# Selective-scan kernel: the running sum y is added by TensorE through the identity, and copied back by ScalarE, in images 1 to 3 as well as in image 0

## The chip, the cores and the metric

The kernel runs on one core of one Trainium2 chip. The metric is the device time in microseconds (us) of one execution, taken as the median of several. Five engines of the core matter: TensorE (PE in the profile, its weight loads PEld), VectorE (DVE), ScalarE (ACT), GpSimd (POOL) and SyncE (SP), which only issues DMAs here. Each engine runs its own instructions in the order of the program; semaphores make one engine wait for another.

## The reference, cut to what matters

Layer 0 is a selective scan over four images of 48 x 48 positions with 256 channels. For each image, each of four directions k (rows, columns, and both reversed) and each of 16 states n, a recurrence runs along the L = 2304 positions, and the four results are added in the order of the positions:

```
dA = jnp.exp(dt_l[..., None] * A)
h  = h * dA + (dt_l * u_l)[..., None] * B_l[:, :, None, :]
y  = jnp.einsum('bkdn,bkn->bkd', h, C_l)
...
ys = ys + Ds.reshape(1, K, d, 1) * xs
y  = ys[:, 0] + ys[:, 2][..., ::-1]        # + directions 1 and 3, transposed
```

Layer norm, a gate and a projection follow, then attention over the tokens, then a long convolution with 16 filters (the "STU"), whose products are matrix multiplications.

## The kernel before, in words

**Scan stage.** Each image b has one scan stage. It is cut into 24 chunks: 4 directions times 6 chunks of CS = 384 positions. A chunk has 8 units (h, q): two halves h of the channels, four groups q of four states. One unit is a tile `s` of 128 partitions x 4 x 384 (partitions hold 32 channels x 4 states). Its steps, with lines of the profile:

- L517 `s = rep * B`: on DVE for five units of a chunk (B is first copied by ACT into a PSUM slot, L509), on POOL for the three units in `POOLED`.
- L526 decay: ACT writes exp(dt * A) into a slot of `ring`, four slots in PSUM (five in image 0), four decays per unit.
- L533 scan: DVE runs the recurrence over 384 positions, four scans per unit; a scan frees its ring slot for a later decay.
- L541 and L543: POOL saves the last column as `carry` and multiplies `s` by C.
- L551: PE sums over the states with the matrix `csum`, for two units at a time; after the four q of a half the bank `y` (one buffer) holds the chunk's result of 128 channels x 384 positions.
- `add_y`: the result goes into `ya` (`yaccs` in the code), the running sum of the image in SBUF. This is what the change touches. There are two per chunk, 48 per image.

**Preparing later chunks.** While a chunk is scanned, `prep` makes dt and dt * u of the next ones: matmuls of PE into ring slots (L421, L438), copies by ACT (L428, L441), softplus by ACT in place (L452, issued for two chunks one behind the other, so in every second chunk), and L474 on DVE, two products `dx = dt * x` of 128 x 384, followed by the DMAs that store and replicate them (L463, L468, SP's queue). Column directions (odd k) read `x` and `ya` with a stride.

**Other work beside the scans.** In image 0 PE makes the mixed filters G (L984). In images 1 to 3 PE runs the STU of the image before: products L1207 into the banks cx and cy, projections L1273; ACT copies the results between (L1223, L1227, L1230, L1231). The function `more` hands this work out in equal shares of columns, in four places per unit; the result copies come 500 columns later in the program.

**Order.** Nothing is planned by a scheduler: the Python loop in `scans` writes the order of every engine by hand. Step s of the loop enters later units, runs the four scans of unit s with shares of the other work between them, and lets POOL multiply unit s - 1. The sums L551 of units s - 3 and s - 2 end a step; `add_y` of a finished half comes in the next step. `fill` issues as many decays as ring slots are free ahead of each scan.

In image 0 the addition was already in the form that the change extends: PE adds `ya` onto the sums through `ident` (L554), and ACT copies the bank back (L561). In images 1 to 3 DVE adds the bank to `ya` (L563).

Of the kernel before, what the change touches and what calls it, by code (L numbers as in the profile page):

```python
# [10 lines left out]
ALU = mybir.AluOpType  # L11
# [10 lines left out]
CS = 384  # L22
SUB = 384
NT = L // P
G4, DL, C4, Q4 = 4, 32, 4, 4
# [35 lines left out]
def hybrid_kernel(ctx: ExitStack, tc: tile.TileContext, a: dict, out: bass.AP):  # L61
# [3 lines left out]
    nc = tc.nc  # L65
# [272 lines left out]
    def in_order(t, k, lo, n):  # L338

        if k % 2 == 0:  # L340
            return t[:, lo // W:(lo + n) // W, :]
        return t.rearrange("p h w -> p w h")[:, lo // H:(lo + n) // H, :]
# [154 lines left out]
    class Unit:  # L497
# [47 lines left out]
        def sum_c(self, ps):  # L545

            ch = self.ch
            if self.q == 0:
                ch.y = ps.tile([P, 512], F32, tag="y", name=f"y{self.name}")
            for g in range(G4):  # L550
                nc.tensor.matmul(ch.y[g * DL:(g + 1) * DL, :CS], csum, self.s[:, g], start=(self.q == 0),  # L551
                                 stop=(self.q == Q4 - 1))
            if ch.b == 0 and self.q == Q4 - 1:
                nc.tensor.matmul(ch.y[:, :CS], ident, in_order(yaccs[ch.b][self.h], ch.k, ch.lo, CS), start=False,  # L554
                                 stop=True, skip_group_check=True)

        def add_y(self):
            ch = self.ch
            v = in_order(yaccs[ch.b][self.h], ch.k, ch.lo, CS)
            if ch.b == 0:  # L560
                nc.scalar.copy(v, ch.y[:, :CS].rearrange("p (r w) -> p r w", w=v.shape[2]))  # L561
                return
            nc.vector.tensor_tensor(v, v, ch.y[:, :CS].rearrange("p (r w) -> p r w", w=v.shape[2]), ALU.add)  # L563

    NCH = L // CS
    POOLED = ((0, 3), (1, 1), (1, 3))
# [50 lines left out]
    def scans(b, chunks, preps, front, sp, back, ring, finish, work, work_cols):  # L617

        units = [Unit(ch, h, q) for ch in chunks for h, q in quads]
        total = len(chunks) * CHUNK_COLS + work_cols  # L620
        done = [0]

        def more(share):

            while done[0] < share * total:
                cols = next(work, None)
                if cols is None:
                    break
                done[0] += cols

        def enter(s):

            if s + 2 < len(units) and units[s + 2].pool:
                units[s + 2].enter(sp.s, ring)
            if 0 <= s + 1 < len(units) and not units[s + 1].pool:
                units[s + 1].enter(sp.s, ring)

        wanted, issued = [], [0]

        def fill(left=0):  # L640

            while wanted and ring.free:
                wanted.pop(0).spread(ring)
            while len(ring.free) > left and issued[0] < G4 * len(units):
                i = issued[0]
                issued[0] += 1
                units[i // G4].decay(i % G4, ring)

        def scan(s, g):
            fill()  # L650
            units[s].scan(g, ring)

        def spread(s):
            if s < len(units) and not units[s].pool:
                wanted.append(units[s])

        def prepare(s):

            ci, j = divmod(s, len(quads))
            for c in range(ci + 1, ci + 5):  # L660
                if c < len(chunks) and 0 <= s - len(quads) * c + LEAD[c % 2] < STEPS[c % 2]:
                    done[0] += next(preps[c]) or 0

        def refill(s, i):

            if 0 <= s < len(units) and s // len(quads) + 1 < len(chunks):
                u, nxt = units[s], chunks[s // len(quads) + 1]
                if u.h == NH - 1:
                    nxt.fetch(i + u.q, front)

        pending = []
        spread(0)
        fill(len(ring.free) - 1)
        enter(-2)
        enter(-1)
        spread(1)
        fill(1)
        for i in range(3 if units[0].ch.b else 0):
            done[0] += next(work)
        for s in range(len(units) + 2):  # L680
            real = s < len(units)
            enter(s)
            prepare(s)
            if real:
                scan(s, 0)
            more((s + 0.25) / len(units))
            next(finish, None)
            if 1 <= s <= len(units):
                units[s - 1].times_c(s >= len(units) - (units[0].ch.b == 0))
            if real:  # L690
                scan(s, 1)
            if pending:
                pending.pop().add_y()
            prepare(s)
            more((s + 0.5) / len(units))
            next(finish, None)
            spread(s + 2)
            if real:
                scan(s, 2)
            more((s + 0.75) / len(units))  # L700
            next(finish, None)
            prepare(s)
            if real:
                scan(s, 3)
            refill(s - 2, Q4)
            refill(s + 1, 0)
            if s >= 2 and units[s - 2].q % 2:
                units[s - 3].sum_c(back.psy)
                units[s - 2].sum_c(back.psy)
                done[0] += 2 * CS  # L710
                if units[s - 2].q == Q4 - 1:
                    pending.append(units[s - 2])
            more((s + 1) / len(units))
            next(finish, None)
        for u in pending:
            u.add_y()
        for _ in work:
            pass
# [898 lines left out]
    for b in range(B):  # L1617
# [3 lines left out]
        if b == 0:  # L1621
            mixed = Stage(tc, "m", "right", two=(2, SB))
            scans(b, *first, front, sp, ps, ring, iter(()), mixture(mixed, ps), MIX_COLS)
            mixed.close()
        else:
            env.append(ps)
            scans(b, *first, front, sp, ps, ring, finish(b - 1), work, STU_COLS)
# [139 lines left out]
```

## Time and profile before

| what | value |
|---|---|
| median of 3 runs | 5423.6 us (5423.21 to 5428.04) |
| profiled execution | 5427.03 us; its span 5425.3 us |
| mean granted TensorE clock | 0.926 |
| busy share of the span | PE 86%, PEld 58%, DVE 80%, ACT 59%, POOL 67% |
| scan stage, first scan to last: image 0 | 111.9 to 1059.3 us |
| scan stage, first scan to last: image 1 | 1295.4 to 2250.8 us |

A row of the profile gives the line, the engine, the operation, the tiles (output <- inputs), the shape and the count; then the busy time in us, the mean of one in ns, and the idle time of the engine just before these instructions with what ended it. A float32 matmul of this kernel stands as two matmul instructions (192 of them would be 96 products); the end of a matmul is modelled. Overlapping instructions of one engine are counted once in busy time. Images 2 and 3 repeat image 1 closely: windows of 834 us in each show the same counts within four instructions on every engine.

### The profile page before, as it was taken

The numbers are of one execution on the slowest core, as the hardware profiler recorded it, in microseconds if no ns is written. First come the engines' busy times: TensorE is split into PE (matmuls) and PEld (weight loads), VectorE is DVE, ScalarE is ACT, GpSimd is POOL, SyncE is SP. The second block draws the span as 40 slices with busy tenths as digits, with TensorE's granted clock in tenths as the row PEclk, the third lists the DMA queues.
The fourth block names the chain that finished last, engine by engine and source line by source line (L and its number), as shares of the span: only waits on it lengthen the run. The fifth ranks groups of instructions, "written<-read, shape, count | busy, mean of one in ns | idle before, by whom it ended". The sixth has DMA issues, their size and how long they took to land. (4 is left out here: it accounts for less than half of the span.)

```text
span 5425.3 us, 71267 instructions
## 1 busy us (share of the span) xinstructions
PE 4658.1 (86%) x23372; PEld 3120.5 (58%) x23372; DVE 4324.9 (80%) x5309; ACT 3210.7 (59%) x6846; POOL 3656.8 (67%) x1881
## 2 busy tenths in 40 slices
PE   4555555599999999998899999898899999989999
PEld 2222222255666666645666666656666667559987
DVE  8999999856999999856999999658999999423211
ACT  3666666546777766456776766457777666432111
POOL 2999999713989999605999999407998999201100
PEclk7777777799999999999999999999999999999999
DMA  4444454404877777406787787227777777136543
GB/s 138 154 162 155 160 171 160 128 27 145 247 260 253 252 260 244 146 31 204 237 264 249 243 272 247 88 78 211 248 246 260 248 260 238 38 83 153 151 142 91
DMA packets 732185, 996.11 MB, mean 184 GB/s; under 512 B 108969, under 2 KB 580649, under 8 KB 731753
## 3 DMA queue, kind: packets, MB, share of 16 engines
q1 hardware_dynamic: 725992, 988.26, 57.6%
q10 hardware_dynamic: 5824, 3.30, 0.3%
q8 instruction: 187, 3.06, 0.2%
q14 instruction: 182, 1.48, 0.1%
HBM read 873.03 MB, written 118.31 MB: 183 GB/s over the span
## 5 line engine op out<-in xcount | busy, mean ns | idle before, releaser
L533 DVE TENSOR_TENSOR_SCAN s<-ring,s 128x385 f32<-128x385 f32 x3072 | 2691.4, 937 | 75.8 <-ACT ring L526 75.4
L543 POOL TENSOR_TENSOR s<-s,bc 128x1536 f32<-128x1536 f32 x763 | 2423.2, 3178 | 96.3 <-DVE s L533 39.9
L526 ACT ACTIVATE ring<-rep,A 128x384 f32<-128x384 f32 x3072 | 1757.8, 584 | 885.5 <-DVE s L517 524.2
L517 POOL TENSOR_TENSOR s<-rep,bc 128x1536 f32<-128x1536 f32 x288 | 994.2, 3452 | 131.9 <-DMA rep<-dtdud 70.9
L517 DVE TENSOR_TENSOR s<-rep,ring 128x1536 f32<-128x1536 f32 x480 | 830.3, 1731 | 34.9 <-ACT ring L509 20.0
L551 PE MATMUL y<-s,csum 128*32 128x384 f32 x6144 | 646.9, 538 | 109.4 <-POOL s L543 88.9
L1207 PE MATMUL cx<-tt,u 128*128 128x252 f32 (+7 forms) x2880 | 622.5, 361 | 124.3 <-ACT cy L1223 123.3
L1207 PEld LDWEIGHTS cx<-tt,u 128*128 128x128 f32 x2880 | 514.9, 195 | 308.0 <-ACT cy L1223 181.3
L1207 PE MATMUL cx<-tt,us 128*128 128x252 f32 (+7 forms) x2880 | 597.6, 352 | 51.5 <-ACT U L1231 49.4
L1207 PEld LDWEIGHTS cx<-tt,us 128*128 128x128 f32 x2880 | 494.6, 191 | 172.6 <-ACT U L1231 73.0
L1207 PE MATMUL cy<-tt,u 128*128 128x252 f32 (+5 forms) x2880 | 588.2, 349 | 0.0
L1207 PEld LDWEIGHTS cy<-tt,u 128*128 128x128 f32 x2880 | 497.2, 192 | 102.6 <-issue 41.1
L984 PE MATMUL G<-M,W 128*128 128x256 f32 (+3 forms) x512 | 222.7, 570 | 259.5 <-ACT W L974 134.7
L551 PEld LDWEIGHTS y<-s,csum 128*32 128x32 f32 x6144 | 166.3, 116 | 457.6 <-issue 259.0
L1273 PE MATMUL pr<-U,G 128*128 128x288 f32 (+4 forms) x1344 | 425.6, 448 | 3.0 <-DMA G<-gd 3.0
L1543 POOL TENSOR_TENSOR t<-s,s 128x512 f32<-128x512 f32 x48 | 63.4, 1320 | 513.8 <-ACT s L1541 513.8
L866 ACT ACTIVATE e<-s,shift 128x512 f32<-128x512 f32 (+1 forms) x360 | 230.2, 643 | 272.1 <-PE s L864 271.7
L864 PE MATMUL s<-xnT 128*128 128x512 f32 (+1 forms) x720 | 339.7, 556 | 23.7 <-ACT xnT L824 12.5
L856 PE MATMUL o<-e,xn 128*128 128x512 f32 (+1 forms) x720 | 336.9, 552 | 0.0
L984 PEld LDWEIGHTS G<-M,W 128*128 128x128 f32 x512 | 111.4, 239 | 364.0 <-ACT W L974 142.1
L1273 PEld LDWEIGHTS pr<-U,G 128*128 128x128 f32 x1344 | 235.0, 192 | 121.8 <-issue 71.4
L541 POOL COPY carry<-s 128x4 f32<-128x4 f32 x640 | 121.0, 189 | 231.9 <-DVE s L533 229.5
(237 smaller groups left out, 5040.6 us busy)
## 6 DMA issues: line engine op xcount, KB each, us to landing
rep<-dtdud SPq DMA_DIRECT2D x768, 384.0 KB
bc<-xdd SPq DMA_DIRECT2D x768, 192.0 KB
tt<-fd SPq DMA_DIRECT2D x144, 577.0 KB
tt<-fd SPq DMA_DIRECT2D x144, 451.0 KB
tt<-fd SPq DMA_DIRECT2D x144, 325.0 KB
dtdud<-dt SPq DMA_DIRECT2D x192, 192.0 KB
dtdud<-dx SPq DMA_DIRECT2D x192, 192.0 KB
t<-fd SPq DMA_DIRECT2D x80, 384.0 KB
```

The costliest lines, as they stand in the source:

```text
L517: eng.tensor_tensor(s, self.ch.rep[self.h][:, :, 1], bt.unsqueeze(1).to_broadcast([P, G4, CS]), ALU.mult)
L526: nc.scalar.activation(ring.body(self.dA[g]), ch.rep[self.h][:, g, 0], AF.Exp, scale=A[:, ch.k, self.h * G4 + g, self.q:self.q + 1])
L533: nc.vector.tensor_tensor_scan(s, ring.decays(i, ch.rev), s, 0.0, ALU.mult, ALU.add)
L541: nc.gpsimd.tensor_copy(carry[:, self.h, self.q].unsqueeze(2), self.s[:, :, end:end + 1])
L543: eng.tensor_tensor(self.s, self.s, ch.bc[Q4 + self.q].unsqueeze(1).to_broadcast([P, G4, CS]), ALU.mult)
L551: nc.tensor.matmul(ch.y[g * DL:(g + 1) * DL, :CS], csum, self.s[:, g], start=(self.q == 0), stop=(self.q == Q4 - 1))
L856: nc.tensor.matmul(po[J][:, :w], xn[:, i], e[:, :w], start=(i == 0), stop=(i == NT - 1))
L864: nc.tensor.matmul(p[:, :w], xnT[:, i * P:(i + 1) * P], xnT[:, 512 * J:512 * J + w], start=True, stop=True)
L866: nc.scalar.activation(e[:, :w], p[:, :w], AF.Exp, bias=shift)
L984: nc.tensor.matmul(p[:, :n], W[:, q if t else 0, i], M[t][:, i].unsqueeze(1).to_broadcast([P, n, C]), start=(t == 0 and i == 0), stop=(t = ...
L1207: nc.tensor.matmul(p4[:, 1:3, v - (hi - at):] if g else p4[:, 0:4:3, v - (hi - at):], x, t[:, :, hi - 1 - at + J * P:end if end >= 0 else ...
L1273: nc.tensor.matmul(o if q else o.rearrange("p f r m -> p r f m"), G, U[n][:, 4 * q:4 * q + 4, v0:v1].rearrange("p (a b) m -> p a b m", a=2 ...
```

## The change

`add_y` of images 1 to 3 takes the form that image 0 has: one more product of PE per half and chunk, of `ya` with the identity onto the bank, and a copy by ACT from the bank to `ya`; the addition by DVE is gone. In images 1 to 3 the place of `add_y` in a step moves from behind scan 1 to behind scan 3. Image 0 stays as it is. The instructions of POOL and the DMAs of SP keep their order.

```diff
-            if ch.b == 0 and self.q == Q4 - 1:
+            if self.q == Q4 - 1:
                 nc.tensor.matmul(ch.y[:, :CS], ident, in_order(yaccs[ch.b][self.h], ch.k, ch.lo, CS), start=False,
                                  stop=True, skip_group_check=True)
 
         def add_y(self):
             ch = self.ch
             v = in_order(yaccs[ch.b][self.h], ch.k, ch.lo, CS)
-            if ch.b == 0:
-                nc.scalar.copy(v, ch.y[:, :CS].rearrange("p (r w) -> p r w", w=v.shape[2]))
-                return
-            nc.vector.tensor_tensor(v, v, ch.y[:, :CS].rearrange("p (r w) -> p r w", w=v.shape[2]), ALU.add)
+            nc.scalar.copy(v, ch.y[:, :CS].rearrange("p (r w) -> p r w", w=v.shape[2]))
...
             if real:
                 scan(s, 1)
-            if pending:
+            if pending and not units[0].ch.b:
                 pending.pop().add_y()
...
             if real:
                 scan(s, 3)
+            if pending:
+                pending.pop().add_y()
             refill(s - 2, Q4)
```

## The prediction

> **What bounds the kernel now.** I read the page first, then busy time by window inside the scan stages, then the waits of each engine, then the timeline where those waits sit. The page names no single bound: DVE 80%, PE 86%, POOL 67% are averages over unlike stages. The change acts in three scan stages of about 955 us, so I take a steady stretch of image 1 and the like-long one of image 0 (columns: PE, PEld, DVE, ACT, POOL busy, clock, DMA share, GB/s):
>
> ```profile
> 150.00:985.00 835.00, 462.63 (x2008) 177.94 (x2006) 801.38 (x822) 569.71 (x1227) 768.60 (x377) 0.75 0.49 162
> 1345.00:2180.00 835.00, 785.09 (x4447) 562.41 (x4445) 809.50 (x865) 596.76 (x1306) 766.49 (x375) 0.98 0.78 252
> ...
> 1782.00:2180.00 398.00, 382.12 (x2104) 271.16 (x2102) 385.85 (x414) 275.68 (x591) 367.40 (x183) 0.98 0.76 253
> ```
>
> In 835 us DVE is busy 97%, PE 94%, POOL 92%. DVE looks like the bound. But image 0, where DVE no longer adds y, does the same POOL work in the same time (377 against 375 instructions), so taking this addition from DVE need not quicken the chunks. The timeline at the end of a chunk shows why:
>
> ```profile
> 1455.59 3.18 POOL L543 TENSOR_TENSOR s<-s,bc 128x1536 f32<-128x1536 f32 x1
> ...
> 1456.90 2.75 DVE L474 TENSOR_TENSOR dx<-dt,xc 128x384 f32<-128x384 f32 x2
> ...
> 1459.58 0.95 DVE L533 TENSOR_TENSOR_SCAN s<-ring,s 128x385 f32<-128x385 f32 x1
> ...
> 1460.59 0.19 POOL L541 COPY carry<-s 128x4 f32<-128x4 f32 x1 [1.82 <-DVE s L533]
> ```
>
> Two L474 need about 1.0 us (530 ns is the shortest), but took 2.75: DVE was held until POOL's product ended at 1458.77. Then POOL idled 1.82 us, because its next unit needs the scan behind L474. Once per chunk DVE thus waits for POOL and POOL for DVE. A chunk costs POOL eight L543 (3.18), three L517 (3.45), up to eight carries (0.19) with their 0.08 us gaps, 37.9 us less some overlap, and this 1.82: about 39.2 us, or 39.7 where the two L474 last 0.8 us each. Image 1 spends 955 / 24 = 39.8. **POOL's chain with this meeting is a floor just below the present pace; DVE's addition is not.**
>
> The waits of that stretch:
>
> ```profile
> POOL carry L541 <- DVE s L533: 45.1, 23, 3.2
> POOL s L543 <- DVE s L533: 11.4, 5, 3.9
> ...
> DVE s L533 <- ACT ring L526: 15.9, 16, 2.3
> DVE ya L563 <- PE y L551: 8.3, 11, 1.9
> ...
> PE cx L1207 <- ACT cy L1223: 31.5, 21, 4.1
> PE cx L1207 <- ACT U L1231: 14.6, 11, 2.9
> ```
>
> POOL waits 56.5 us for DVE. The meeting explains 21 x 1.82 = 38, plus about 11 chunks x 0.53 for the slow L474 = 44. Only some 12 us per image are late DVE.
>
> **What the Trainium skill says.** "SBUF — State Buffer", section "Who interferes with whom", says that a VectorE instruction with two SBUF inputs contends with a GpSimd instruction that reads SBUF, one with at most one does not, and PE and ACT never wait. The trace agrees: L474 (two SBUF inputs) stretches to 2.28 us at 1456.90 and 3.26 at most, while L563, with y in PSUM, stays within 0.52 to 0.87. So the new copy and product join no such queue, and the removed addition stood in none. "ScalarE activation tables: per-element evaluation and per-set limits", section "What a function is on this engine", puts two functions of different table sets one load of 1283 ns apart; the trace has exactly that, twice around each pair of softplus, and DVE starves behind it:
>
> ```profile
> 1495.03 1.28 ACT L526 ACT_TABLE_LOAD   x1
> ...
> 1496.94 1.81 DVE L533 TENSOR_TENSOR_SCAN s<-ring,s 128x385 f32<-128x385 f32 x2 [2.11 <-ACT ring L526]
> ```
>
> **The change part by part,** per image of 48 additions: the groups of both forms (x144 are three images, x48 is image 0), and the product in image 0's timeline.
>
> ```profile
> L563 DVE TENSOR_TENSOR ya<-ya,y 128x384 f32<-128x384 f32 x144 | 98.5, 684 | 31.2 <-PE y L551 30.9
> L561 ACT COPY ya<-y 128x384 f32<-128x384 f32 x48 | 31.0, 646 | 43.4 <-PE y L554 43.3
> ```
>
> ```profile
> 714.69 0.91 PE L554 MATMUL y<-ya,ident 128*128 128x384 f32 x2
> 715.44 1.45 PE L984 MATMUL G<-M,W 128*128 128x384 f32 x4
> ```
>
> DVE loses 48 x 0.684 = 33 us of instructions and 31 / 3 = 10 us of waits for y. Not all shortens the chunk: the ceiling is the 12 us in which POOL waits beyond the floor. In every second chunk DVE starves on the softplus before it reaches L474, and arriving earlier only lengthens that wait; by the timeline about a third of the 12 us lies there. **Gain: 8 us.**
>
> PE gains a product from 714.69 to 715.44, 0.75 us at full clock: 48 x 0.75 = 36 us. It fills PE's own waits for ACT (46 us in the stretch), which shrink when PE is later. In the second half (1782 to 2180) those are 15.7 us and the 20 products cost 15.0: full. The planner's column count does not include them, so nothing is taken away in exchange. Estimate for lag left uncovered there: **2 us**, from 0 to 15.
>
> ACT gains 48 x 0.646 = 31 us, inside 238 us of idle. Two things behind it count. First, queued decays: the place behind scan 3 comes about 1.5 us later in ACT's order than DVE's old one (one scan, one decay of 0.58), y comes 0.75 later, so waits for y, up to 1.9 before, stay near 1.2, and two or three scans of decays are ahead. Only behind the softplus is none ahead: the changed order puts the copy between the first and second decay, which makes the second some 0.3 us late, ten times per image, half of it hidden by L474's own hold: **1.5 us**, from 0 to 8. Second, results of L1207 arrive up to 0.75 us later at ACT, which already waits 43 us for them (21.7, 13.7 and 8.0 for L1230, L1223, L1227); where this delays a softplus, DVE pays. Four such delays of 0.75: **3 us**, from 0 to 10.
>
> At the image's end the last y must pass the product too before the means L746: **0.8 us**, the copy itself (0.82 to 0.84) equalling the addition (0.83). The single bank y is free one step before its next sums, at no cost; if ACT held it, PE would wait (5.8 us once in image 0). `add_y` issues no DMA, so its move passes nothing on SP or POOL.
>
> Sum: -8 + 2 + 1.5 + 3 + 0.8 = -0.7 us per image, -2 in all. Against the profiled 5427.0 that is 5425; the median of the runs lies 3.4 lower, so I predict **5421.5 us**.
>
> **The rivals.** *A, the relief counts in full:* PE's waits swallow the products and nothing moves on ACT. For it: 46 us of PE waiting, 238 of ACT idle. Against it: the second half and the softplus. Gain 8 to 12 per image: about 5394, and 5387 at the very best (3 x 12).
>
> *B, PE becomes the bound, slower:* place, the second half of each scan stage, where conv products stand nearly back to back. If its 15.7 us of waiting are forced (PE waits there for a copy that hangs on a decay, that hangs on a scan), the products add 15 us per image; ACT, queued behind later conv results, passes it to the ring and DVE. With a gain of 5 in the first half, +10 per image: 5454. It decides from the point where less than about half of that waiting can be filled. At worst no wait is filled anywhere, 3 x 36: 5531. Against it: DVE tolerates PE's lateness by two scans.
>
> *C, the change does less than it says:* image 0 untouched and PE's clock already 0.98, so no further effect there; this merges with my forecast.
>
> **How the numbers follow.** A measurement of this kernel can tell about 0.2%, 11 us, from no change. Forecast (gain and losses cancel, own range 5406 to 5440): 0.40, of which 0.28 within 11 us and 0.06 on either side. A: 0.24, all faster but 0.01. B: 0.36, all slower but 0.02. Sums: faster 0.29, same 0.31, slower 0.40. The range must reach into A and B: 5396 leaves out A's far half (0.1), 5466 leaves out B beyond a third of the 3 x 36 us (0.1).
>
> **What would show it right or wrong.** Right: L563 gone; L554 four times as many; per chunk still 39.2 to 39.8 us; POOL's wait per chunk still 1.82 or 2.35; L474 held longer, as in image 0 (up to 3.26). PE waits for ACT fall by most of 36 us. A: POOL's waits in 1345 to 2180 fall towards 44 us and the stage to 943. B: PE over 98% in the second half, ACT's waits for PE (43 us) doubled, the ring waits of DVE (15.9) doubled, POOL's waits above 65. The forecast is wrong if a scan stage moves by more than 6 us.

## The result, and the profile after

The changed kernel takes **5475.8 us** (median of 4 runs, 5474.05 to 5479.49) against 5423.4 for the kernel before beside it: 1.0094 times as long, with a 95% interval of 1.0081 to 1.0106. It is slower by 52 us; the forecast was 5421.5 and its range ended at 5466. Its form is close to that of rival B. The profiled execution has a span of 5472.3 us at a mean granted clock of 0.932, so the loss is not one of the clock (0.926 before).

The same two windows of image 1, of the kernel after (columns: PE, PEld, DVE, ACT, POOL busy with counts, clock, DMA share, GB/s):

```profile
1345.00:2180.00 835.00, 803.21 (x4471) 568.42 (x4472) 775.42 (x815) 611.26 (x1332) 758.66 (x371) 0.99 0.78 250
1782.00:2180.00 398.00, 389.81 (x2117) 273.37 (x2117) 368.94 (x389) 280.72 (x600) 361.14 (x179) 0.99 0.76 250
```

In the second half PE is now busy 389.8 of 398 us, 98%, while DVE and POOL are less busy than before: POOL did 371 instructions in 835 us where it had done 375. DVE and POOL do less work in the same time and PE is fuller; ACT is busier too, by its new copies.

The waits in 1345 to 2180 of the kernel after (us in total, number, longest), in the order POOL, DVE, ACT, PE:

```profile
POOL carry L541 <- DVE s L533: 52.8, 20, 5.1
POOL s L543 <- DVE s L533: 11.2, 5, 6.0
...
DVE s L533 <- ACT ring L526: 41.4, 32, 3.9
...
ACT cy L1222 <- PE cx L1206: 35.2, 23, 3.6
ACT U L1229 <- PE cx L1206: 30.4, 26, 3.5
ACT U L1226 <- PE cy L1206: 13.7, 16, 2.0
ACT ya L560 <- PE y L554: 1.5, 2, 1.2
...
PE cx L1206 <- ACT cy L1222: 16.4, 11, 3.8
PE cx L1206 <- ACT U L1230: 10.8, 6, 2.7
```

(Lines behind the change stand one lower than before: L1206 was L1207.) PE's waits for ACT fell from 46 to 27 us. But ACT's waits for PE rose from 43 to 79, DVE's waits for a decay from 15.9 to 41.4, and POOL's for a scan from 56.5 to 64.0. Not all of the longer waits for a decay goes with the loss: in the first experiment below, without the product and without a loss, they are 31.5 us already, so only some 10 us come with the product. Over the whole of the three scan stages POOL's waits for scans rose from 204.0 to 248.8 us, 45 of the 51 us by which the stages grew. One place in the timeline of the kernel after shows how the lateness travels:

```profile
1533.17 0.91 PE L554 MATMUL y<-ya,ident 128*128 128x384 f32 x2
...
1536.99 0.56 ACT L1222 COPY cy<-cx 128x504 f32<-128x504 f32 x1 [3.62 <-PE cx L1206]
...
1537.56 0.59 ACT L526 ACTIVATE ring<-rep,A 128x384 f32<-128x384 f32 x1
...
1538.26 0.96 DVE L533 TENSOR_TENSOR_SCAN s<-ring,s 128x385 f32<-128x385 f32 x1 [2.64 <-ACT ring L526]
...
1541.18 1.58 DVE L474 TENSOR_TENSOR dx<-dt,xc 128x384 f32<-128x384 f32 x2
...
1543.77 3.18 POOL L543 TENSOR_TENSOR s<-s,bc 128x1536 f32<-128x1536 f32 x1 [6.00 <-DVE s L533]
```

The same place in the kernel before:

```profile
1534.38 0.56 ACT L1223 COPY cy<-cx 128x504 f32<-128x504 f32 x1 [2.97 <-PE cx L1207]
...
1535.64 2.66 DVE L533 TENSOR_TENSOR_SCAN s<-ring,s 128x385 f32<-128x385 f32 x3 [0.38 <-ACT ring L526]
...
1540.81 3.18 POOL L543 TENSOR_TENSOR s<-s,bc 128x1536 f32<-128x1536 f32 x1 [3.88 <-DVE s L533]
```

PE makes the new product ahead of the long convolution's products. ACT, whose next instruction in order is the copy L1222 of such a result, waits 3.62 us for it. The decay L526 stands behind that copy and the trace shows no wait of its own, so the scan waits 2.64 us, and POOL at the end of the row 6.00 us. The three waits were there before, at 2.97, 0.38 and 3.88 us: the product lengthens them. Against the kernel before, PE is 1.97 us later at the sums ahead of the product and 2.72 us later behind it; the copy comes 2.61 us later, the scan 2.62, and POOL's product 2.96, while POOL's last work ahead of its wait had started only 0.82 us later.

Where in a stage the time went, from the starts of the scans in the traces (mean per image of images 1 to 3, us; a stage has 24 chunks):

| kernel | chunk 0 | 1 to 11 | 12 to 21 | 22 and 23 | stage |
|---|---|---|---|---|---|
| before | 47.2 | 439.5 | 396.9 | 71.8 | 955.4 |
| after | 48.2 | 443.1 | 404.3 | 76.7 | 972.3 |
| after without the product (first experiment below) | 47.5 | 437.0 | 396.4 | 71.6 | 952.5 |

The stage moved by 17 us, where the prediction called itself wrong from 6. 16.9 us per image are 51 in all: the whole loss lies in the three scan stages, and 12 of the 17 us behind chunk 11: 7.4 in chunks 12 to 21, where PE had been fullest (96%), and 4.9 in the last two.

### The profile page after: what moved, and what is told of

It reads as the page before. It is cut to its first block, busy times and chain, and to the rows that moved or that the text cites. A ratio compares the mean times of both kernels' runs of the same rounds, so it can differ in the third digit from the quotient of the medians.

```text
span 5472.3 us, 72019 instructions
## 1 busy us (share of the span) xinstructions
PE 4752.1 (87%) x23660; PEld 3164.1 (58%) x23660; DVE 4241.2 (78%) x5165; ACT 3279.5 (60%) x6990; POOL 3657.6 (67%) x1881
## 5 line engine op out<-in xcount | busy, mean ns | idle before, releaser
L526 ACT ACTIVATE ring<-rep,A 128x384 f32<-128x384 f32 x3072 | 1755.0, 584 | 706.0 <-DVE s L517 422.3
L551 PE MATMUL y<-s,csum 128*32 128x384 f32 x6144 | 634.6, 530 | 114.4 <-POOL s L543 82.2
L1206 PE MATMUL cx<-tt,u 128*128 128x252 f32 (+7 forms) x2880 | 606.3, 355 | 80.2 <-ACT cy L1222 79.4
L1206 PEld LDWEIGHTS cx<-tt,u 128*128 128x128 f32 x2880 | 512.6, 193 | 250.8 <-ACT cy L1222 120.4
L1206 PE MATMUL cx<-tt,us 128*128 128x252 f32 (+7 forms) x2880 | 599.3, 353 | 40.3 <-ACT U L1230 38.3
L1206 PEld LDWEIGHTS cx<-tt,us 128*128 128x128 f32 x2880 | 504.3, 194 | 157.4 <-ACT U L1230 57.4
L1206 PE MATMUL cy<-tt,u 128*128 128x252 f32 (+5 forms) x2880 | 581.4, 346 | 0.0
L1206 PEld LDWEIGHTS cy<-tt,u 128*128 128x128 f32 x2880 | 498.3, 191 | 100.3 <-issue 42.0
```

Of the source, the lines that this page charges most:

```text
L526: nc.scalar.activation(ring.body(self.dA[g]), ch.rep[self.h][:, g, 0], AF.Exp, scale=A[:, ch.k, self.h * G4 + g, self.q:self.q + 1])
L1206: nc.tensor.matmul(p4[:, 1:3, v - (hi - at):] if g else p4[:, 0:4:3, v - (hi - at):], x, t[:, :, hi - 1 - at + J * P:end if end >= 0 else ...
```

## The experiments

**Theory 1**: the product on PE costs the time, since PE's waits for ACT could not be filled, and its lateness passes through ACT's order to DVE and POOL. **Rival**: the copy on ACT costs it, by delaying decays. Each experiment was timed beside the kernel before, whose median then lay between 5423.7 and 5425.2 us; times of different experiments are compared on that ground. The first four ask which part it is.

### The copy alone

`add_y` and its place are those of the changed kernel; images 1 to 3 get no product, so the old y is left out of their sum.

```diff
-            if self.q == Q4 - 1:
+            if ch.b == 0 and self.q == Q4 - 1:
```

> The changed kernel without the product by TensorE in images 1 to 3: ScalarE still copies the bank to ya behind scan 3, VectorE adds nothing, so in those images the old y is left out of the sum. Theory 1 (the product makes TensorE late; ScalarE waits for the later convolution results and with it the decays): with TensorE's load as before, the relief of VectorE remains alone, 5385 to 5412 us. Theory 2 (the copy on ScalarE starves the ring of decays): nearly all of the loss stays, 5460 to 5476 us. Theory 3 (the place of the copy): like theory 2.

Measured: 5418.7 us, ratio 0.9989 [0.9981, 0.9998]. Without the product the loss is gone: the 48 copies per image on ACT cost next to nothing, and the product costs 57 us. The range expected of theory 1 was missed all the same, by 7 us, because the relief of DVE brings less than it took.

### The product alone, copied by DVE in the old place

The kernel before with the product in all images:

```diff
-            nc.vector.tensor_tensor(v, v, ch.y[:, :CS].rearrange("p (r w) -> p r w", w=v.shape[2]), ALU.add)
+            nc.vector.tensor_copy(v, ch.y[:, :CS].rearrange("p (r w) -> p r w", w=v.shape[2]))
```

> The product by TensorE in all images, but in images 1 to 3 VectorE copies the bank back, in its old place behind scan 1; ScalarE has no new work. Theory 1: TensorE is as late as in the changed kernel and VectorE is not relieved, 5465 to 5510 us. Theory 2: VectorE works as before and ScalarE too, 5415 to 5432 us. Theory 3: as theory 2.

Measured: 5486.7 us, 1.0113 [1.0098, 1.0128]. The loss stays although ACT has no copy, so the rival falls. By the medians it is 11 us worse than the changed kernel, though the two intervals overlap. DVE itself now stands behind the product (waits in 1345 to 2180 of this kernel):

```profile
DVE ya L563 <- PE y L554: 30.2, 27, 3.8
```

That wait was 8.3 us before. DVE's waits for a decay are 15.7 us here, as in the kernel before (15.9). The product's lateness thus reaches DVE mainly by another way than in the changed kernel and costs as much: that the product costs the time is shown, while the way through ACT's order is read from the trace of the changed kernel.

### No addition at all

The kernel before without L563 in images 1 to 3: what freeing DVE can bring at most.

> The kernel before without the addition in images 1 to 3 (y is not added to ya at all): no product, no copy, nothing on VectorE. This measures what the relief of VectorE can bring at most. The floor of the prediction (GpSimd's chain with one meeting per chunk) says 8 to 12 us per image: 5385 to 5400 us. If VectorE itself is the bound (its 97% in the window), it is 33 us of additions plus 10 us of waits per image: 5295 to 5330 us.

Measured: 5416.9 us, 0.9983 [0.9976, 0.9990]: a gain of 7 to 9 us in the whole kernel, though DVE lost 98.5 us of instructions. The groups show where the rest went, first in the kernel before:

```profile
L533 DVE TENSOR_TENSOR_SCAN s<-ring,s 128x385 f32<-128x385 f32 x3072 | 2691.4, 937 | 75.8 <-ACT ring L526 75.4
...
L474 DVE TENSOR_TENSOR dx<-dt,xc 128x384 f32<-128x384 f32 x192 | 171.7, 934 | 4.6 <-ACT dt L452 4.6
```

and in this kernel:

```profile
L533 DVE TENSOR_TENSOR_SCAN s<-ring,s 128x385 f32<-128x385 f32 x3072 | 2679.8, 938 | 116.8 <-ACT ring L526 116.5
...
L474 DVE TENSOR_TENSOR dx<-dt,xc 128x384 f32<-128x384 f32 x192 | 211.5, 1141 | 4.6 <-ACT dt L452 4.6
```

L474 lasted 934 ns in the mean before and lasts 1141 here, with the same shapes: 40 us more busy time. The scans wait 117 us for decays instead of 75. This fits a DVE that reaches L474 earlier, is held there longer, and runs into the ring. So DVE's addition did not set the pace. The gain is smaller even than the floor of the prediction allowed: 5385 to 5400 us were expected of it.

### The old place

The changed kernel with the copy behind scan 1:

```diff
-            if pending and not units[0].ch.b:
+            if pending:
                 pending.pop().add_y()
...
-            if pending:
-                pending.pop().add_y()
```

> The changed kernel with the copy by ScalarE behind scan 1 in images 1 to 3 too, as image 0 has it. Theory 1: the place matters little or makes it worse, as ScalarE then waits for y itself: 5470 to 5520 us. Theory 3 (the place behind scan 3, just behind the restart after softplus, is what costs): 5424 to 5450 us. Theory 2: within 10 us of the changed kernel.

Measured: 5483.4 us, 1.0106 [1.0091, 1.0121], some 8 us more than the changed kernel, with overlapping intervals. In its window ACT waits 30.0 us for the product (`ACT ya L560 <- PE y L554: 30.0, 25, 4.1`), against 1.5 in the place behind scan 3. The move takes this wait away; that it saves time is not shown beyond the noise.

### How much of the product: half, and twice

In images 1 to 3 the product covers 192 of 384 columns (the rest of the old y is left out), or is issued twice (the old y then counts double).

```diff
-                nc.tensor.matmul(ch.y[:, :CS], ident, in_order(yaccs[ch.b][self.h], ch.k, ch.lo, CS), start=False,
+                n = CS if ch.b == 0 else CS // 2
+                nc.tensor.matmul(ch.y[:, :n], ident, in_order(yaccs[ch.b][self.h], ch.k, ch.lo, n), start=False,
```

```diff
+                for i in range(2 if ch.b else 1):
+                    nc.tensor.matmul(ch.y[:, :CS], ident, in_order(yaccs[ch.b][self.h], ch.k, ch.lo, CS), start=False,
+                                     stop=True, skip_group_check=True)
```

> The changed kernel with the product over half of the columns (192 of 384) in images 1 to 3, so the old y is left out for the other half. TensorE then has 0.36 to 0.4 us per product for 0.75. Theory 1b with TensorE full throughout: half of the 57 us, 5443 to 5451 us. Theory 1a or TensorE full only in some chunks: the first half of the load is cheaper, as waits take it up: 5424 to 5440 us.

> The changed kernel with the product issued twice in images 1 to 3 (ya then counts double in the sum). From none over half to one product the time went 5419, 5442, 5476. If TensorE is then full in every chunk, the second product passes on with its whole 0.75 us x 144 = 108 us: 5570 to 5590 us. If half of every load is still taken up by waits: some 57 to 70 us more, 5530 to 5548 us.

Measured: half 5441.8 us, 1.0033 [1.0023, 1.0043]; twice 5586.1 us, 1.0301 [1.0284, 1.0319]. The table sets them beside the load on PE. A product's load is read from the trace as the time from its start to PE's next product; it is given here for all three images. Waits are those in 1345 to 2180, summed from the answers as above.

| product | load on PE | time | ACT for PE | DVE for the ring | POOL for DVE |
|---|---|---|---|---|---|
| none (copy alone) | 0 | 5418.7 | 41.8 | 31.5 | 53.9 |
| half | 83 | 5441.8 | 62.5 | 37.4 | 59.4 |
| whole (the change) | 152 | 5475.8 | 79.3 | 41.4 | 64.0 |
| twice | 291 | 5586.1 | 114.7 | 60.2 | 93.0 |

The first 83 us of load cost 23 us, 0.28 per us; the next 69 cost 34, 0.49 per us; the last 139 cost 110, 0.79 per us. Half a product already costs time, so the load is not free up to a point, and each further us costs more, four fifths of it in the last step. The half lies between the two ranges that were expected of it; the doubled product lies in the range for a PE that is full in every chunk. The windows of the kernel with two products:

```profile
1345.00:2180.00 835.00, 805.77 (x4416) 562.57 (x4416) 745.01 (x784) 590.27 (x1289) 729.75 (x356) 0.99 0.76 241
1782.00:2180.00 398.00, 391.57 (x2091) 272.19 (x2084) 352.61 (x371) 269.35 (x578) 345.43 (x169) 1.00 0.74 241
```

PE's busy time hardly rises over the 803.2 and 389.8 of the change: it was nearly full already there, and now POOL's count falls from 371 to 356.

### A lighter PE, before and after

Part of the projection L1273 (its second product group, for 9 of 16 filters) is left out, in the kernel after and in the kernel before. L1273's busy time falls from 425.6 to 319.1 us in the latter:

```diff
-                for v0, v1, x in parts(w, extra):
+                for v0, v1, x in () if q and (k % 2 or k in (4, 12)) and k < KF - 1 else parts(w, extra):
```

> The changed kernel with other work taken from TensorE instead: in images 1 to 3 the projection of the second filter bank is left out for 9 of 16 filters (part of the sum is missing in the output), some 36 us of matmuls per image, as much as the products are; they stand spread over the stage, away from the products. If what counts is the sum of TensorE's load: the loss is gone, 5412 to 5432 us. If it is the place of the products: it stays, 5455 to 5476 us.

> The kernel before with the same projections left out. If TensorE was a bound before already and its load passes on at the same rate of about half (57 us for 108 us): 5424 less some 40 to 55, 5370 to 5385 us. If the floor of the prediction holds (GpSimd's chain with one meeting per chunk, some 12 us per image under the time before): not under 5387 us, and rather 5400 to 5420.

Measured: after 5450.5 us, 1.0048 [1.0033, 1.0063]; before 5432.8 us, 1.0014 [1.0007, 1.0021]. The same relief brings 25 us after the change and none before it (there it is 8 us slower; why was not tested). The waits of PE in the second of these, in 1345 to 2180:

```profile
PE cx L1207 <- ACT cy L1223: 45.0, 28, 4.2
PE cx L1207 <- ACT U L1231: 18.6, 16, 3.1
```

They sum to 64 us where the kernel before has 46: PE without the work just waits longer. So PE did not bound the kernel before, and with the product it does in part; this and the table of doses carry theory 1. Both ranges for the kernel after were missed, as were those for the kernel before. With the lighter PE the change still costs 18 us. The relief, some 107 us of L1273, is less than the 152 us of the products, so a rest was due; whether that is all of the reason stays open.

### Is it the distance of the copies, or the count?

If PE is late, results could be taken later: `LATER`, the distance of the result copies in columns, from 500 to 750, in both kernels. Or the product's columns could be counted, so that `more` hands out less work beside it.

```diff
-LATER = 500
+LATER = 750
```

```diff
-        total = len(chunks) * CHUNK_COLS + work_cols
+        total = len(chunks) * (CHUNK_COLS + NH * CS) + work_cols
...
+                    done[0] += CS
```

> The changed kernel with LATER = 750 for 500: ScalarE's copies of the convolution results stand 250 columns later in its order. The runs so far put the loss on the product by TensorE (57 us with it, none without). Theory 1a (ScalarE meets those copies too early, because TensorE is late by the product, and its decays stand behind them): the copies come when the result is there, ScalarE's waits for it (79 us in the window) fall by half, and 15 to 40 us come back: 5435 to 5460 us. Theory 1b (TensorE has no room left: throughput): TensorE now waits longer for the copies in turn, no gain: 5470 to 5495 us.

> The kernel before with LATER = 750 for 500, as control. Theory 1a: ScalarE's waits for convolution results there (43 us in the window) fall, but they cost little: 5412 to 5426 us. Theory 1b: TensorE waits longer for the copies: 5424 to 5445 us.

> The changed kernel, with the columns of the product counted in the shares by which other work is handed to TensorE, so that less of it follows directly on a product. Theory 1a: a smoother load, up to 15 us back: 5460 to 5476 us. Theory 1b: the sum of the work is the same, within 6 us of the changed kernel: 5470 to 5482 us.

Measured: later in the kernel after 5496.0 us, 1.0127 [1.0110, 1.0144]; later in the kernel before 5464.9, 1.0072 [1.0057, 1.0087]; counted 5466.5, 1.0075 [1.0057, 1.0092]. The idea that a later copy relieves the chain fell: it costs 20 us after and 41 us before, above every range given for it. ACT's waits for PE hardly fall (79.3 to 77.7 in the window after), and PE waits longer for its banks (27 to 35 us). In the kernel before ACT's waits for PE fall from 43.4 to 36.5 us, but PE's for ACT rise from 46.1 to 52.2 and DVE's for y from 8.3 to 18.8: PE and ACT hand banks to and fro, and there the wait that one is spared turns up with others. Counting gives some 9 us back, though its interval overlaps that of the change.

### What the product costs: columns, rows, and its place

The trace of the kernel after shows that products are not alike. The first product here belongs to a column direction (the last chunk of k = 1) and 20 us later to a row direction:

```profile
1795.19 1.54 PE L554 MATMUL y<-ya,ident 128*128 128x384 f32 x2
1796.56 1.69 PE L1206 MATMUL cx<-tt,u 128*128 128x254 f32 x8
...
1814.74 0.91 PE L554 MATMUL y<-ya,ident 128*128 128x384 f32 x2
1815.48 1.66 PE L1206 MATMUL cy<-tt,u 128*128 128x252 f32 x8
```

From its start to the next product it takes 1.37 us in the one and 0.74 in the other; the medians over an image are 1.36 and 0.75. The kernel before had shown it too, in the column directions of image 0:

```profile
373.23 1.54 PE L554 MATMUL y<-ya,ident 128*128 128x384 f32 x2
374.59 1.68 PE L984 MATMUL G<-M,W 128*128 128x512 f32 x4
```

In column directions the product reads `ya` with a step of 48 values, 192 bytes. The Trainium skill, page "SBUF — State Buffer", section "Door 1: The DMA port swizzle (why `[64,N]` ≈ `[32,N]`)", says that SBUF has lines of 16 bytes and that every access that crosses to a new line pays. The experiment reads the same values in runs of 8 neighbours, and lets the output carry the step instead:

```diff
+                y, v = ch.y[:, :CS], in_order(yaccs[ch.b][self.h], ch.k, ch.lo, CS)
+                if ch.b and ch.k % 2:
+                    y, v = y.rearrange("p (w h) -> p h w", h=H), v.rearrange("p w h -> p h w")
+                nc.tensor.matmul(y, ident, v, start=False, stop=True, skip_group_check=True)
...
```

> The changed kernel, but in the column directions of images 1 to 3 the product reads ya in rows of 8 adjacent values and writes the bank with a stride, in place of reading every 48th value. In the trace of the changed kernel the column products take 1.36 us, the row products 0.75. If the stride of the read is that price: all products 0.75, the load falls from 152 to 108 us, and between the half product (76 us of load, 5442) and the whole (152, 5476) that is 5450 to 5462 us. If the stride on either side costs the same: 5470 to 5480 us.

Measured: 5460.4 us, 1.0058 [1.0043, 1.0073]. A product of a column direction (the same chunk stands at 1635.06 in the kernel after, with 1.35 us to its next) in this kernel:

```profile
1634.08 0.91 PE L557 MATMUL y<-ya,ident 128*128 128x384 f32 x2
1634.82 0.82 PE L1208 MATMUL cx<-tt,u 128*128 128x254 f32 x4
```

The step in the read was the whole surcharge, as the page lets one expect: the median is now 0.75 us in column directions as in rows, the load falls from 152 to some 110 us, and 15 us of the time come back.

The change made only in row directions, or only in column directions (the others keep DVE's addition in the old place). The edit of the first, against the kernel before; the second has `== 1` for `== 0` and the reverse in the place:

```diff
-            if ch.b == 0 and self.q == Q4 - 1:
+            if self.q == Q4 - 1 and (ch.b == 0 or ch.k % 2 == 0):
...
-            if ch.b == 0:
+            if ch.b == 0 or ch.k % 2 == 0:
                 nc.scalar.copy(v, ch.y[:, :CS].rearrange("p (r w) -> p r w", w=v.shape[2]))
...
-            if pending:
+            if pending and (not units[0].ch.b or pending[0].ch.k % 2 != 0):
                 pending.pop().add_y()
...
             if real:
                 scan(s, 3)
+            if pending:
+                pending.pop().add_y()
```

> Product and copy only in the row directions of images 1 to 3; the column directions keep VectorE's addition in its old place. Load of TensorE 24 x 0.75 x 3 = 54 us. If the load's sum decides: 5430 to 5440 us. If the products of the column directions are the loss (1.36 us in one piece): 5419 to 5428 us.

> Product and copy only in the column directions of images 1 to 3. Load 24 x 1.36 x 3 = 98 us. If the load's sum decides: 5448 to 5458 us. If the column products are the loss: 5466 to 5476 us.

Measured: rows only 5447.5 us, 1.0036 [1.0024, 1.0049]; columns only 5453.8 us, 1.0043 [1.0028, 1.0058]. Beside the kernel before (5424.7) that is 23 and 29 us by the medians, which add up to the whole 52. The rows bring 54 us of load and the columns 98. The rows thus seem dearer for their load, and their kernel lies above both ranges that were expected of it. But the intervals, 7 to 8 us to either side, allow the same cost for each us of load, so this pair does not show that the place of a product matters as well.

The product set ahead of the first sums of a half, at q = 0, instead of behind the last, and this together with reading in rows:

```diff
+            if ahead and self.q == 0:
+                nc.tensor.matmul(ch.y[:, :CS], ident, in_order(yaccs[ch.b][self.h], ch.k, ch.lo, CS), start=True,
+                                 stop=False, skip_group_check=True)
...
```

In images 1 to 3 (`ahead`) all sums then add onto it, and the product behind the last sums is gone.

> The changed kernel with the product issued ahead of the first pair of sums of a half, not behind the second: the same load on TensorE, 10 us earlier, and y ready 0.75 us sooner behind its last sums. If the load counts wherever it stands: within 10 us of the changed kernel, 5466 to 5486 us. If the loss comes from the product standing behind the sums at the end of a step, where other work of TensorE waits: 5425 to 5455 us.

> Both at once: the column products read in rows of 8, and every product of images 1 to 3 stands ahead of the first pair of sums. If load (20 us of the loss by interpolation) and place (17 us measured) are separate causes that add: 5432 to 5446 us. If the place counted only because of the long column products: 5450 to 5460 us. Not under the kernel before either way.

Measured: first 5458.9 us, 1.0066 [1.0051, 1.0081]; first and in rows 5438.2 us, 1.0026 [1.0019, 1.0032]. The place gives 17 us back, which lies between the two ranges expected of it, and both together 38. Part of the 17 is again price: compared in the trace over all groups of image 1, a product behind the last sums adds 749 ns (rows), while ahead of the first it adds 645, since the convolution's product before it then ends its turn in 213 ns instead of 305 and the product itself counts 737. In column directions it is 1359 against some 1280. That is 13 us less load in three images, for 17 us gained, which the intervals (7 to 8 us to either side) can't tell apart. What else the place does stays open. In the last kernel ACT waits 62.2 us for PE, and DVE 35.6 for the ring: the best of the changed forms, and still 13 us slower than the kernel before. No version tried that computes all of it beats the kernel before.

## Why the prediction was wrong, step by step

**Right in kind, too large in size: the relief of DVE.** It counts little, as the prediction said. It took 8 us per image with a ceiling of 12; measured with no addition at all it is 2.4 to 3 (7 to 9 us in all). L474 is held by GpSimd, as the Trainium skill, "SBUF — State Buffer", section "Who interferes with whom", told, and without the addition it is held longer (1141 ns in the mean for 934): some 13 us per image. Longer waits for decays took another 14 of the 43 us that the sum counted as freed. The forecast's own signs asked for a longer hold in the changed kernel; there L474 fell to 908 ns.

**Right: the copy on ACT.** 1.5 us per image were taken for it. The kernels without product, with and without the copy, differ by 1.8 us in all (5418.7 and 5416.9), less than their intervals, and in the changed kernel ACT's waits for y were 1.5 us in the window.

**Wrong, the step that failed: "Estimate for lag left uncovered there: 2 us", with "it fills PE's own waits for ACT".** The prediction set 36 us of products against 46 us of PE's waits and let one vanish in the other. Measured, the product costs 57 us, 19 per image, against the 2 + 3 + 0.8 that the sum had for all its effects on PE. A wait of PE for ACT in this pair of banks was not free time here: with the product, PE's wait shrank by 19 us, not by most of 36, but ACT's wait for PE grew (46 to 27, and 43 to 79), and behind ACT's wait stand the decays. The prediction named that channel in rival B and in "queued behind later conv results", gave it 3 us as "four such delays", and took as the argument against it that DVE tolerates PE's lateness by two scans. The dose table shows that it is passed on from the first half of a product. Image 0, where the same form runs, could not warn of it: PE was busy 463 of 835 us there. The runs split the 17 us per image that were measured into about -3 for the relief, 0.6 for the copy and 19 for the product.

**Wrong: the price "48 x 0.75 = 36 us".** It came from one row direction's product. (The granted clock there was 0.81, not full; row products of images 1 to 3 took the same 0.75 at 0.98.) Half of the products cost 1.36 us: 24 x 0.75 + 24 x 1.36 = 50.6 us per image. The term was 15 us per image too low; the runs put 5 us per image of time on that (15 us back when read in rows). The rest, 14 us per image, would have come at 0.75 too, so that the price alone would not have saved the forecast.

**Missing: the last two chunks.** "At the image's end ... 0.8 us" was for the way behind the last scan, and no lengthening shows there: from the last scan of images 1 and 2 to the first of the next it was 235.8 and 235.7 us before, and is 233.6 and 236.2 after. But the last two chunks became 4.9 us longer, for which the sum had no term. They are back at 71.6 without the product, at 71.9 with it in row directions alone, and at 74.2 when it reads in rows.

**Rival B** came out in mechanism, and its signs nearly: PE at 97.9% in the second half where it asked for over 98, ACT's waits 79 of the 86 that "doubled" asks, POOL's waits 64.0 where it asked for over 65. The ring waits more than doubled, but they nearly did so without the product too. Its size, 30 us for all three images, was too small: it let only the second half lose. The first half (chunks 1 to 11) lost 3.6 us per image too, where B had a gain of 5.

## What to carry to other kernels

Before moving work to an engine with idle time, ask who waits in order behind that engine's results: where two engines hand banks to each other, the idle time of one can be the other's working time, and filling it then moves the wait instead of using it up. Price an added instruction in every access pattern that it will have, not from the first example in the trace. And before paying for relief, remove the relieved work altogether in one run: here it showed a ceiling of 0.2% for the relief of VectorE, before anything was paid for it.

## What the runs showed of the hardware

- A float32 product of 128 x 384 whose moving operand is read from SBUF with a step of 192 bytes took 1.36 us from its start to the next, against 0.75 when the same values were read in runs of 8. The output in PSUM then carried the step of 192 bytes, at no cost that shows (749 ns as for the output in order).
- The same product added 0.65 us ahead of the sums with `csum` and 0.75 behind them, in row directions: the order of the products changed the cost by 0.1 us. Why was not tested.
- Taking 98.5 us of work from VectorE gave 40 us to another instruction of VectorE with two inputs in SBUF, beside GpSimd's products (L474 from 934 to 1141 ns in the mean).
